# Graph network with edge lists on one core: when the edge stages fetch and put, and which queues carry four of the transfers

## The chip, the cores and the metric

The kernel runs on one core of a Trainium2 chip. The metric is the device time of one execution in microseconds. Three runs of the kernel before took 3205.14, 3216.49 and 3216.53 us; the median is 3216.49 us.

The engines are TensorE (PE, with PEld for its weight loads), VectorE (DVE), ScalarE (ACT), GpSimd (POOL) and SyncE (SP). SP computes nothing here; it issues transfers. A transfer is issued by an engine, in the order of that engine's instructions, so an instruction that has to wait holds up the transfers behind it.

## The reference

32 entries x of 512 nodes by 256 features pass through four layers. `adj` is a 512 by 512 matrix in which about 1.6% of the cells and the diagonal are not zero; it is the same for all entries. Layers 0 and 3 are the same function with other weights:

```
pre_u, pre_v = h @ W1[:d], h @ W1[d:]
S   = sigmoid(relu(pre_u[u] + pre_v[v] + b1) @ W2 + b2)      # 512 x 512 pairs (u, v)
a_t = (S * adj).T @ h
m_t = (adj @ h) * h
z   = beta1*h + beta2*(a_t @ Wa + ba) + beta3*(m_t @ Wm + bm)
```

Layer 1 is `z + relu(adj @ z @ W.T + b)`. Layer 2 is attention: `feats = y @ W1.T`, one number f1 per node, `coefs = softmax(leaky_relu(f1[i] + f1[j]) + adj)`, and `coefs @ feats + bias2 + y`.

S is wanted only where `adj` isn't zero, since it is multiplied by `adj`. This is what the kernel uses.

## The kernel before, in words

The kernel counts the cells of `adj` and takes `sparse_path` where they fit into fixed lists, as they do here. The 32 entries are worked on in 8 groups of four (`NB = 4`, t = 0 to 7). Each group passes through these pieces of work, each of which is a Python generator that yields between its parts:

- `first` (layer 0, four entries in turn): loads h (512 KB), transposes it on PE (`turned`), writes the transposed entry hT to `xT` in device memory, and calls `pre` four times an entry, on blocks of 128 nodes. One `pre` multiplies by W1 on PE, adds b1 on DVE (L548), copies the other half on ACT (L549), computes the pair (u, u) of the diagonal on DVE (L551, L552), and sends the block `puv`, 256 KB, to a table in device memory (L556). The send is held back by one block (`settle`).
- `edges` (layer 0 or 3): the pairs (u, v) of all four entries. There are 36 items of 128 pairs. For an item, GpSimd gathers 128 rows of 4 KB from the table by an indirect transfer (`fetch`, L581) into `rows`, a ring of five buffers. DVE adds `mine` to it, the other end of the pair (L653), and then, for each of the four entries, applies relu, multiplies by W2 and sums (L666). Every fourth item exp on ACT and the rest of the sigmoid on DVE follow; then each item's values of S are scattered by GpSimd into `cells` in device memory (`put`, L575, one an item). `cells` is in two halves; puts into the same half follow each other's landing. S on the diagonal leaves through two transfers of SP (L605). The first fetches (`lead` of them: 3, or with spare buffers 4 in the first stage and 5 in the last) stand in front of the items in one piece, without a yield between them; puts that are left after the last item stand in one piece behind it.
- `middle` (layers 0, 1 and 2): `load` brings S back from `cells` as a dense matrix, four transfers of 1 MB on SP (L688) into the tiles `SA0`. For each entry the sums of layer 0 (L801 and after), layer 1 (whose last addition on DVE, L877, gives yT), the attention of layer 2, the result transposed to `x2T` (L879) and, transposed back on PE and copied by ACT, as `x2` (L891, two transfers an entry), and `pre` for layer 3, which fills layer 3's table.
- `last` (layer 3): S again through `load` (tiles `SA3`), products with Wa (`hWa`), with `adj` (`mhT`), and the sums (L948, L957, L960) to the output.

The order of work is written down in `sparse_path` as a list of streams: each generator has a stretch of time, in units of one group's period, and shares of it. `weave` (L442) sorts all pieces by these planned times and runs the generators in that order, which is the order in which instructions are recorded. Streams of the kind "fill" (`first`, `last`) aren't run at their time but held in a list, and taken from it where `middle` says that PE has room. From t = 2 on, `first` of a group is planned at start − 0.8 to start − 0.54, its layer 0 `edges` at start − 0.53 to start − 0.05, `middle` from start to start + 1, layer 3's `edges` from there for 0.48, and `last` at end + 0.52 to end + 1.2. A scheduler then gives each engine its own list, and may move an instruction past others that it doesn't depend on. So in a steady period DVE works through the edges of layer 0 of the next group, then those of layer 3 of this one, while PE does `middle`, `first` and `last`.

The table of layer 0's edges must be complete before the first gather of `edges`, and S must be scattered completely before `load`.

Of the kernel before, what the change touches and what calls it, by code (L numbers as in the profile page):

```python
# [16 lines left out]
P = 128  # L17
N = 512
D = 256
NC = N // P  # L20
# [10 lines left out]
LINES = PANELS * P  # L31
LEAD = 3
CELLS = HALF * N
ITEMS = NC * OWN + 2 * PANELS
# [378 lines left out]
class Sparse:  # L413
# [28 lines left out]
    def weave(self, streams):  # L442

        order = []
        for k, (_, shares, a, b, _) in enumerate(streams):
            at = 0.0
            for j, share in enumerate(shares):
                order.append((a + (b - a) * at / sum(shares), k, j))  # L450
                at += share
        due, running = [], set()

        def run(k, j):
            g, shares = streams[k][:2]
            room = next(g, None)
            if j == len(shares) - 1:
                for _ in g:
                    raise AssertionError("more pieces than told")
            return room  # L460

        def fill(upto):
            while len(due) > upto:
                run(*due.pop(0))

        for _, k, j in sorted(order):
            kind, end = streams[k][4], len(streams[k][1]) - 1
            if kind == "fill":
                due.append((k, j))
                fill(HELD if running else 0)  # L470
                continue
            if kind == "main" and j == 0:
                running.add(k)
            elif j == 0 and kind != "free":
                fill(0)
            if run(k, j) and due:
                fill(len(due) - (1 if len(due) < HELD // 2 else 2))
            if kind == "main" and j == end:
                running.remove(k)
        fill(0)  # L480
# [104 lines left out]
    def edges(self, g, spare=()):  # L585
# [6 lines left out]
        ready, fetched = [], {}  # L592
        lead = LEAD + len(spare) - 1 if spare else LEAD
        tags = [None] * 5 + list(spare)
# [3 lines left out]
        def own_1():  # L598
# [3 lines left out]
            for q in range(2):  # L602
                diagonal = g.cells[q][q * HALF : q * HALF + HALF * (N + 1), :]
                diagonal = diagonal.rearrange("(c p a) b -> p c a b", p=P, a=N + 1)[:, :, 0, :]
                nc.sync.dma_start(diagonal, g.self_s[:, 2 * q : 2 * q + 2, :])  # L605

# [36 lines left out]
        for n in range(lead):  # L643
            fetch(n)
        yield

# [29 lines left out]
        for _, f in todo:  # L676
            f()
        while ready:
            put()
        yield  # L680

    def load(self, g, layer):

        tiles = []
        for c in range(NC):
            t = self.act.tile([P, N, NB], F32, name=f"SA{layer}", bufs=NC)
            cells = g.cells[c // 2][c % 2 * P * N : (c % 2 + 1) * P * N, :]
            self.nc.sync.dma_start(t.rearrange("p v b -> p (v b)"), cells.rearrange("(p v) b -> p (v b)", p=P))  # L688
            tiles.append(t)
# [26 lines left out]
    def first(self, g, i):  # L716
# [8 lines left out]
        for b in range(NB):  # L725
            ahead = load(b + 1) if b < NB - 1 else None
            hT = self.turned(h, "hT0", "hT")
            yield
            self.nc.sync.dma_start(self.xT[i + b], hT)
            yield from self.pre(g, b, hT)  # L730
# [55 lines left out]
    def middle_one(self, g0, g3, b, i, SA, keep, given):  # L786
# [96 lines left out]
        for c in range(0, NC, 2):  # L883
# [6 lines left out]
            nc.scalar.copy(x2, by_two(pt))  # L890
            nc.sync.dma_start(self.x2s[i][:, c : c + 2, :], x2)  # L891
            yield
# [93 lines left out]
def even(n):  # L986
    return [1.0] * n
# [3 lines left out]
FIRST, LAST, AHEAD, BEHIND = even(NB * 5 + 1), even(NB * 8 + 1), even(NB * 4 + 1), even(NB * 4 + 1)  # L991
EDGES = [4.0] + even(ITEMS + 1)

# [17 lines left out]
def sparse_path(ctx, m, counts, xr, outr, B):  # L1011
# [4 lines left out]
    streams = [  # L1016
        (sp.setup(), even(NC + 1 + NC + 2 * (OWN // 2 + 1) + 1), -0.40, -0.295, ""),
        (sp.setup_behind(), even(2 * (OWN // 2 + 1) + 2 * PANELS + 4), -0.285, -0.16, ""),
        (sp.setup_rest(), even(7), -0.26, -0.20, ""),
        (sp.zeros_behind(), even(2), 0.15, 0.2, ""),  # L1020
    ]
    for t in range(last + 1):
        g0, g3 = Group(sp, m.g0, f"0_{t}"), Group(sp, m.g3, f"3_{t}")
        start, end = (max(0.0, k - 0.47) for k in (t, t + 1))
        behind = (end, end + 0.48), (end + 0.52, end + 1.2)
        if t == 0:
            early = (-0.385, -0.30), (-0.292, -0.02)
        elif t == 1:
            early = (-0.28, -0.06), (0.02, start - 0.04)
        else:  # L1030
            early = (start - 0.8, start - 0.54), (start - 0.53, start - 0.05)
        if t == last - 1:
            behind = (end, end + 0.46), (end + 0.6, end + 1.08)
        if t == last:
            end -= 0.2
            behind = (end, end + 0.46), (end + 0.29, end + 0.45)
        streams += [
            (sp.first(g0, t * NB), FIRST, *early[0], "fill"),
            (sp.edges(g0, ("yT", "mhT3") if t == 0 else ()), EDGES, *early[1], ""),
            (sp.middle(g0, g3, t * NB), middle_shares(t == 0), start, end, "main"),  # L1040
            (sp.edges(g3, ("yT", "h1", "hT1") if t == last else ()), EDGES, *behind[0], "free"),
        ]
        if t == 0:
            streams.append((sp.middle_before(g0, 0), AHEAD, -0.15, -0.03, ""))
        if t < last:
            streams.append((sp.last(g3, t * NB), LAST, *behind[1], "fill"))
        else:
            streams.append((sp.last_before(g3, t * NB), AHEAD, *behind[1], ""))
            streams.append((sp.last_behind(g3, t * NB), BEHIND, end + 0.5, end + 0.6, ""))
    sp.weave(streams)  # L1050
# [237 lines left out]
```

## Time and profile before

| | |
|---|---|
| three runs | 3205.14, 3216.49, 3216.53 us; median 3216.49 |
| profiled execution, its own time | 3222.47 us |
| its span | 3220.7 us |
| mean granted TensorE clock | 0.924 |
| PE busy | 2741.7 us (85%) |
| DVE busy | 2351.1 us (73%) |
| POOL busy | 1472.2 us (46%) |
| ACT busy | 980.4 us (30%) |
| moved by DMA | 679.37 MB, mean 211 GB/s |
| gathers of rows (L581) and scatters of S (L575) on POOL | 554 of mean 1.21 us, 576 of mean 1.18 us |
| S loads on SP (L688) | 64 of 1 MB, median 7.0 us from issue to landing |
| table writes on SP (L556) | 256 of 256 KB, median 4.7 us |
| xT written (L729), x2T written (L879), on SP | 32 and 32 of 512 KB, median 6.8 and 4.5 us |

A line of the profile's table of groups reads: program line, engine, operation, tile written, an arrow, tiles read, how many; then busy microseconds and the mean of one in nanoseconds; then how long the engine stood idle just before such an instruction and what ended the largest part of that. In the table of waits, the three numbers are idle microseconds, how many waits, and the longest. In the chain, each row has its start, its length, and who it was; it is followed back from the last instruction, each step to whatever released it.

Stages can be told apart in the trace by the gathers: a stage begins when the first rows are fetched after its table has been written. The layer 0 stages begin at about 649, 1024, 1401.8, 1774.3, 2150 and 2522 us, the layer 3 stages at about 850, 1223, 1600, 1975, 2349 and 2720 us. Before 505 us lie the building of the lists and the first group's start, and from 3015 us the last group's end.

### The profile page before, as it was taken

How to read it: one execution, taken by the hardware profiler on the slowest of the kernel's cores; microseconds unless marked ns; L12 is line 12 of the kernel's file. 1: busy time of each engine (PE TensorE's matmuls, PEld its weight loads, DVE VectorE, ACT ScalarE, POOL GpSimd, SP SyncE). 2: the span in 40 equal slices, each digit the busy share in tenths (PEclk: the TensorE clock that was granted, in tenths of full speed). 3: DMA queues.
4: the chain of work that ended last, by engine and by line, in shares of the span. 5: the costliest groups of instructions: out<-in, count | busy, mean ns of one | idle time of the engine just before them, and what ended most of it. 6: DMA issues, size and time to landing. Idle time of an engine off the chain costs nothing.

```text
span 3220.7 us, 32267 instructions
## 1 busy us (share of the span) xinstructions
PE 2741.7 (85%) x8645; PEld 1652.4 (51%) x8646; DVE 2351.1 (73%) x7594; ACT 980.4 (30%) x2309; POOL 1472.2 (46%) x1248
## 2 busy tenths in 40 slices
PE   6356888889997998979998899979989799989947
PEld 3123444446553665545654565535655466545636
DVE  7677837988595967969497785959678694962672
ACT  4352333322233222322223222332223222232441
POOL 1565504546263644627264462636445372540371
PEclk9677988999998999989999999989999899999979
DMA  8876526886777656786577766776567775751663
GB/s 274 295 241 214 174 92 214 260 254 194 223 226 252 206 190 207 233 255 220 176 227 246 223 202 206 229 247 201 193 210 241 258 225 176 223 169 39 201 211 111
DMA packets 302716, 679.37 MB, mean 211 GB/s; under 512 B 52672, under 2 KB 170944, under 8 KB 294336
## 3 DMA queue, kind: packets, MB, share of 16 engines
q0 software_dynamic: 111168, 338.90, 33.9%
q1 hardware_dynamic: 186224, 334.68, 31.6%
q10 hardware_dynamic: 5136, 3.68, 0.4%
q8 instruction: 70, 1.15, 0.2%
q14 instruction: 118, 0.97, 0.1%
HBM read 531.12 MB, written 146.01 MB: 210 GB/s over the span
## 4 chain that ended last, share of the span: by engine, by line
PE 35%; DVE 27%; DMA 12%; issue 5%; ACT 2%; POOL 1%; SPq 0%; DVEq 0%; ACTq 0%; POOLq 0%
PE pst L43 24%; DVE rows L666 9%; DVE rows L653 8%; DMA rows<-table,iv 5%; PE pst L948 4%; DMA table<-puv 3%; PE pst L801 2%; DMA cells<-s,cell 2%; PE pst L899 2%; PE pst L957 1%; DVE ex L855 1%; DMA mine<-table,iu 1%; PE pst L808 1%; DVE both L551 1%; DVE puv L548 1%
## 5 line engine op out<-in xcount | busy, mean ns | idle before, releaser
L581 POOL DMA_INDIRECT rows<-table,iv x554 | 671.2, 1212 | 1060.3 <-DMA table<-puv 392.8
L575 POOL DMA_INDIRECT cells<-s,cell x576 | 678.6, 1178 | 587.0 <-DMA cells<-s,cell 348.2
L653 DVE TENSOR_TENSOR rows<-rows,mine 128x1024 f32<-128x1024 f32 x554 | 667.6, 1217 | 185.5 <-DMA rows<-table,iv 158.0
L666 DVE SCALAR_TENSOR_TENSOR rows<-rows,L_gnn_W2bc 128x256 f32<-128x256 f32 x2016 | 749.4, 416 | 0.4
L43 PE MATMUL pst<-adj,h 128*128 128x512 f32 x1024 | 452.6, 593 | 0.0
L43 PE MATMUL pst<-L_gnn_Wa,hT 128*128 128x256 f32 x1024 | 274.1, 423 | 131.6 <-DMA hT<-xT 75.9
L43 PE MATMUL pst<-w_L_gnn_W,hT 128*128 128x512 f32 x512 | 259.2, 644 | 79.0 <-ACT hT L536 74.0
L43 PEld LDWEIGHTS pst<-L_gnn_Wa,hT 128*128 128x128 f32 x1024 | 216.5, 217 | 176.4 <-issue 104.6
L43 PEld LDWEIGHTS pst<-adj,h 128*128 128x128 f32 x1024 | 192.9, 191 | 221.2 <-issue 218.8
L43 PE MATMUL pst<-w_L_gnn_W,yT 128*128 128x512 f32 x512 | 240.5, 623 | 44.9 <-DVE yT L877 44.9
L43 PE MATMUL pst<-eT,feats 128*128 128x512 f32 x512 | 233.8, 611 | 9.4 <-ACT eT L900 9.4
L43 PE MATMUL pst<-adjT,zW 128*128 128x512 f32 x512 | 225.0, 593 | 0.0
L948 PE MATMUL pst<-hWa,SA 128*128 128x256 f32 x896 | 217.2, 398 | 0.0
L948 PEld LDWEIGHTS pst<-hWa,SA 128*128 128x128 f32 x896 | 213.8, 328 | 6.0 <-issue 3.3
L549 ACT COPY puv<-pst 128x256 f32<-128x256 f32 x256 | 94.7, 372 | 391.3 <-DVE puv L548 367.7
L548 DVE TENSOR_TENSOR puv<-pst,bc_L_gnn_b 128x256 f32<-128x256 f32 x256 | 107.0, 418 | 137.6 <-PE pst L43 81.9
L43 PEld LDWEIGHTS pst<-w_L_gnn_W,hT 128*128 128x128 f32 x512 | 101.9, 207 | 191.5 <-issue 94.2
L801 PE MATMUL pst<-flat,hWa 128*128 128x512 f32 x448 | 197.2, 593 | 1.3 <-DVE both L551 1.3
L43 PEld LDWEIGHTS pst<-w_L_gnn_W,yT 128*128 128x128 f32 x512 | 102.4, 201 | 175.2 <-issue 110.1
L770 ACT COPY flat<-SA 128x512 f32<-128x512 f32 x128 | 134.7, 1124 | 182.6 <-PE pst L43 111.4
L899 PE MATMUL pst<-ident,ex 128*128 128x128 f32 x512 | 97.1, 329 | 105.7 <-DVE ex L860 59.5
L566 ACT ACTIVATE s<-s,L_gnn_nb 128x16 f32<-128x16 f32 (+2 forms) x176 | 53.5, 304 | 411.4 <-DVE rows L666 399.6
(165 smaller groups left out, 3696.4 us busy)
## 6 DMA issues: line engine op xcount, KB each, us to landing
table<-puv SPq DMA_DIRECT2D x256, 256.0 KB, 4.7
SA<-cells SPq DMA_DIRECT2D x64, 1024.0 KB, 7.0
h<-in_x_dram SPq DMA_DIRECT2D x64, 512.0 KB, 6.1
mine<-table SPq DMA_DIRECT2D x64, 512.0 KB, 5.4
hT<-xT SPq DMA_DIRECT2D x36, 512.0 KB, 4.6
h<-x2s SPq DMA_DIRECT2D x36, 512.0 KB, 5.3
xT<-hT SPq DMA_DIRECT2D x32, 512.0 KB, 6.8
x2T<-yT SPq DMA_DIRECT2D x32, 512.0 KB, 4.5
```

Source lines behind the costliest of these rows:

```text
L43: nc.tensor.matmul(out, lhsT, rhs, start=(n == 0), stop=(n == len(pairs) - 1))
L548: nc.vector.tensor_tensor(puv[:, 0, :], pp[:, 0:D], w["b1bc"], ALU.add)
L549: nc.scalar.copy(puv[:, 1, :], pp[:, D:])
L566: self.nc.scalar.activation(t, t, AF.Exp, bias=w["nb2"], scale=-1.0)
L575: self.nc.gpsimd.indirect_dma_start(out=g.cells[half], out_offset=bass.IndirectOffsetOnAxis(ap=at, axis=0), in_=s, in_offset=None)
L581: self.nc.gpsimd.indirect_dma_start(out=rows, out_offset=None, in_=g.table, in_offset=bass.IndirectOffsetOnAxis(ap=at, axis=0))
L653: nc.vector.tensor_tensor(rows, rows, other, ALU.add)
L666: nc.vector.scalar_tensor_tensor(part, part, 0.0, w["W2bc"], ALU.max, ALU.mult, accum_out=at)
L770: self.nc.scalar.copy(flat[:, r, :], SA[r][:, :, b])
L801: nc.tensor.matmul(pz, hWa[:, r, cs], flat[:, r, :], start=(r == 0), stop=False)
L899: nc.tensor.transpose(pt[:, js], ex[:, js], self.m.ident)
L948: nc.tensor.matmul(pz[:, k * D : (k + 1) * D], SA[r][:, cs, b], hWa[:, r, :], start=(r + k == 0), stop=False)
```

## The change

1. `edges` yields after each of the first fetches, and after each of the puts that are left at its end (`TAIL` of 6), so that `weave` gives each a planned time of its own (`edge_times`): the first fetches of a stage are planned between the last items of the stage before, the last puts between the first items of the next.
2. With spare buffers, `lead` is 5 in the first and in the last stage.
3. `first` of a group is planned 0.06 of a period earlier, and `last` from end + 0.56 to end + 1.13 instead of end + 0.52 to end + 1.2.
4. The diagonal's two transfers (L605) and the S loads (L688) are issued by GpSimd instead of SP.
5. hT is written to `xT` (L729), and x2 (L891), by ScalarE instead of SP.

`weave` now takes the list of planned times of each stream; `spread` computes it from shares as before. The line numbers in the text are those of the kernel before.

```diff
+LEAD_AT_ENDS = 5
+TAIL = 6
...
-        lead = LEAD + len(spare) - 1 if spare else LEAD
+        lead = LEAD_AT_ENDS if spare else LEAD
...
-                nc.sync.dma_start(diagonal, g.self_s[:, 2 * q : 2 * q + 2, :])
+                nc.gpsimd.dma_start(diagonal, g.self_s[:, 2 * q : 2 * q + 2, :])
...
         for n in range(lead):
             fetch(n)
-        yield
+            yield
...
         for _, f in todo:
             f()
+        for _ in range(TAIL - 1):
+            put()
+            yield
         while ready:
             put()
         yield
...
-            self.nc.sync.dma_start(t.rearrange("p v b -> p (v b)"), cells.rearrange("(p v) b -> p (v b)", p=P))
+            self.nc.gpsimd.dma_start(t.rearrange("p v b -> p (v b)"), cells.rearrange("(p v) b -> p (v b)", p=P))
...
-            self.nc.sync.dma_start(self.xT[i + b], hT)
+            self.nc.scalar.dma_start(self.xT[i + b], hT)
...
-            nc.sync.dma_start(self.x2s[i][:, c : c + 2, :], x2)
+            nc.scalar.dma_start(self.x2s[i][:, c : c + 2, :], x2)
...
-EDGES = [4.0] + even(ITEMS + 1)
+def edge_times(ahead, a, b, behind, lead=LEAD):
+    step = (b - a) / ITEMS
+    first = [ahead + j * min(step, (a - ahead) / lead) for j in range(lead)]
+    return first + spread(even(ITEMS), a, b) + spread(even(TAIL), b, behind)
...
-        behind = (end, end + 0.48), (end + 0.52, end + 1.2)
...
+            first = spread(FIRST, -0.385, -0.30)
+            edges0 = edge_times(-0.292, -0.27, -0.03, -0.02, LEAD_AT_ENDS)
...
-            early = (start - 0.8, start - 0.54), (start - 0.53, start - 0.05)
+            first = spread(FIRST, start - 0.86, start - 0.6)
+            edges0 = edge_times(start - 0.552, start - 0.505, start - 0.06, start - 0.04)
+        edges3 = edge_times(end + 0.003, end + 0.05, end + 0.48, end + 0.54)
+        behind = end + 0.56, end + 1.13
...
-            behind = (end, end + 0.46), (end + 0.29, end + 0.45)
+            edges3 = edge_times(end + 0.003, end + 0.02, end + 0.45, end + 0.46, LEAD_AT_ENDS)
+            behind = end + 0.29, end + 0.45
```

## The prediction

> **What bounds the kernel now.** I read first the page's busy shares and chain.
>
> ```profile
> PE 2741.7 (85%) x8645; PEld 1652.4 (51%) x8646; DVE 2351.1 (73%) x7594; ACT 980.4 (30%) x2309; POOL 1472.2 (46%) x1248
> PE 35%; DVE 27%; DMA 12%; issue 5%; ACT 2%; POOL 1%; SPq 0%; DVEq 0%; ACTq 0%; POOLq 0%
> ```
>
> No engine bounds alone: PE and DVE take turns, joined by DMA latency. A group recurs every 373 us (an `edges` stage for layer 0 starts at 1401.8, 1774.3, 2150). So second I took busy time in 15 us stretches of one such start (columns: sum and count for PE, PEld, DVE, ACT, POOL; granted clock; DMA share; GB/s).
>
> ```profile
> 1730.00:1745.00 15.00, 12.95 (x43) 7.32 (x42) 11.68 (x48) 4.64 (x13) 7.04 (x7) 0.89 0.35 91
> 1745.00:1760.00 15.00, 7.06 (x18) 3.30 (x18) 7.01 (x22) 5.64 (x13) 3.42 (x3) 0.69 0.87 316
> 1760.00:1775.00 15.00, 14.27 (x53) 8.56 (x52) 7.26 (x27) 6.36 (x15) 0.66 (x1) 0.96 0.87 273
> 1775.00:1790.00 15.00, 5.64 (x14) 2.43 (x13) 3.88 (x10) 4.09 (x4) 4.10 (x5) 0.83 1.08 274
> 1790.00:1805.00 15.00, 15.00 (x36) 6.82 (x36) 12.88 (x47) 3.34 (x8) 4.29 (x3) 0.83 0.72 229
> ```
>
> From 1745 to 1790 both engines are half idle. Third, the chain through it:
>
> ```profile
> 1736.90 6.28 PE pst L43 x12
> ...
> 1743.35 8.07 DMA table<-puv
> 1751.51 0.42 DVE puv L548
> ...
> 1769.44 4.63 DMA table<-puv
> 1774.07 0.26 issue
> 1774.34 12.48 DMA rows<-table,iv
> 1786.84 1.24 DVE rows L653
> ...
> 1788.88 0.68 DVE yT L877
> 1789.60 8.19 PE pst L43 x12
> ```
>
> The last item of the stage before ends at 1737.8. The next stage's first must wait for `first` to write its table (to 1774.1), then for a gather (12.5 us). The gap is 49 us. Inside it DVE stalls for a `puv` buffer, because the table write behind the S loads lands after 8.07 us instead of the page's 4.7. At its end PE waits 9.4 us for the second x2T half (L877), queued on DVE behind that first item. Fourth, the waits:
>
> ```profile
> POOL cells L575 <- DMA cells<-s,cell: 348.2, 155, 8.4
> DVE puv L548 <- DMA table<-puv: 55.3, 14, 8.8
> SPq L688 <- DMA cells<-s,cell: 325.0, 30, 26.1
> ```
>
> Scatters to one half queue behind each other's landing. SP stands 325 us at S loads that wait for scatters. The other start (layer 3, 1600 us) is different: from 1481 to 1600 the chain is PE without a break, so idle DVE there costs nothing.
>
> [...] DMA share is 1.08 at 1775 with SP and POOL both feeding it. [...] So S loads leave the table writes' queue and enter the gathers'. The page's queue table shows q0 and q1 apart[...]. [...]
>
> **The change, part by part.** The order in which the built kernel issues tells more than the diff. Per group, against before:
>
> 1. *`first` earlier.* DVE has 5 blocks of `pre` left after the last item instead of 10. Five blocks of three 0.42 us operations (L548, L551, L552), 6.3 us, move ahead of that item; two sums additions (L960, 0.68 us each) leave. So the last item comes 5 us later, DVE and PE both being full there.
> 2. *The gap.* One of two batches is gone, with its buffer stall (6.5 us on DVE). Last item to last block: turned batch, 4 blocks at 1.72 us of PE (6.9 for 16 records) and softmax in between, some 14 us; table write 4.6: table ready 18 us after the last item, an estimate. But POOL must pass its last scatters first. In the built order they still stand ahead of the first fetches, and now three of the four S loads with them; the third waits for the last landing. Before, the four serial scatters began 4.1 us after the last item and the last began at 20.1. S loads now in the same ring may slow them, a wait on the scatter before the first S load adds 1 to 4 us. I take the fetch at 20 to 24 after the last item (36.5 before), so POOL and not the table gates it. Landing: 7.6 us at the quiet start (1600.35), 12.5 here; I take 10, with an S load just ahead. First item at 30 to 34 instead of 49: gain 15 to 19, central 17.8.
> 3. *x2T behind three items.* Before, one addition stood between the two halves. Now three additions (1.22 us each), ten of L666 (0.35 apart) and the first half precede the second half: 3.7 + 3.5 + 0.7, and its own 0.7; PE resumes 8.5 us after the first item starts, not 2.8: +5.7.
> 4. *`last` earlier.* Half a batch of sums, 16 records of L948 (3.7 us) and a few of L957 (0.2 each), moves from the new group's first batch into the batch that ends `middle`, PE-bound: +4.4; DVE running ahead takes back about 2.5 of the PE waits on softmax (L860, 11 us a group). Net +1.9.
> 5. *Diagonals on POOL.* Two per start, ahead of the fetches at the quiet start. POOL shows no plain DMA; the nearest row is the 1.0 us scatter. They are ready at 1598.0 and the table lands at 1600.1: 0.3 us, at most 3 if each takes 2. S loads likewise 1 to 2 us, behind idle POOL; without that idle time, 8 us a group.
> 6. *hT and x2 from ACT.* 12 issues a group at SP's 0.35 to 0.5 us: 5 us on an engine 30% busy. Some stand before the next `puv` copy[...]: 0.5 to 2 us, I take 1.2. SP gains the time; its waits hide behind PE and DVE otherwise.
> 7. *Tail spread, fetches spread*: mostly undone by the issue order, 0 (−1 to +1).
> 8. *Lead 5 instead of 4 in the first stage*: DVE waits 32 us for gathers before 520 us; a quarter, −8 (0 to −15). The last stage already has 5. At the end the S loads follow the last scatters through one queue: +6 (2 to 10).
>
> Group: +5 −17.8 +5.7 +1.9 +0.3 +1.2 = −3.7. Six starts: −22; ends −2: −24. The profiled execution (3222.5, span 3220.7) would become 3198; the median of the runs shown, 6 us lower at 3216.5, 3192.
>
> **Rivals.** *A, the forecast (0.45)*: the shorter gap outweighs what is put in front of x2T and PE. For: 49 us of half-idle engines. Against: it is a difference of large terms.
>
> *B, an even trade (0.20)*: PE's work per group is unchanged and its idle time only some 38 of 373 us; the buffer stall goes and the x2T wait grows by as much. The gap gains 14: ±0, 3216.
>
> *C, slower (0.30)*: POOL's queue becomes the bound at the layer 0 start. S loads of 1 MB each put themselves between the last serial scatters and ahead of the gathers. Before, scatters beside S loads took 5.5 and 6.7 us to land:
>
> ```profile
> 1747.46 0.96 POOL L575 DMA_INDIRECT cells<-s,cell  x1 [4.59 <-DMA cells<-s,cell]
> 1754.18 1.42 POOL L575 DMA_INDIRECT cells<-s,cell  x1 [5.76 <-DVE puv L548]
> ```
>
> If three take 7 and the S load before the fetch 4 us, the fetch starts at 30 and lands at 42: gain 7, group +7, six +42, ends +8: 3266. It decides once the first item comes later than 35 us after the last one (gain below 14). Against: the puts' loads overlap in the old order as well.
>
> *D, it does not do what it says (0.05)*: fetches keep behind the puts, and the batch moved forward only shifts the last item: within 0.5%.
>
> **How the numbers follow.** The runs shown spread by 0.35%, and 0.5%, 16 us, is about what a measurement can tell. A alone spans 3140 to 3210: gains of 23 (quiet landing, table as gate) to 15. Of A 0.43 lies below 3200; of B and D 0.06 below, 0.14 within, 0.05 above; C has 0.01 below, 0.02 within, 0.27 above, with A's other 0.02 within. So faster 0.50, same 0.18, slower 0.32. The range 3138 to 3270 takes in C at its likely size and A at its best; A's own is 3140 to 3210.
>
> **What would show it.** In the changed profile: the time from the last L653-type addition of one stage to the first of the next at a layer 0 start, 30 to 34 us (above 35 is C); `DVE puv <- DMA table` well below 55; SP's wait at S loads gone and POOL waiting at them instead; the PE wait for x2T at 12 to 15 us, not 9.4; no longer gap at the layer 3 start. The prediction is wrong if POOL's S loads take several us each, if DVE starves for rows inside the stages because gathers share their ring[...].

## The result and the profile after

The kernel after takes 3212.62 us (median of 12 runs, 3206.76 to 3220.60); the kernel before, run beside it, 3215.51 us (12 runs, 3203.09 to 3221.36). The ratio is 1.000, 95% interval 0.9985 to 1.0015: no difference. The forecast was 3192 us.

The profiled execution of the kernel after spans 3216.7 us, that of before 3220.7. In both, the work is cut by the first gather of each edge stage into a start (to the third layer 0 stage), four whole groups, and an end:

| us | before | after | difference | forecast |
|---|---|---|---|---|
| first gather of the layer 0 stage at 1000 us | 1024.2 | 1001.4 | −22.8 | −8 |
| four groups from there (one group) | 1498.3 (374.6) | 1497.8 (374.5) | −0.5 (−0.1) | −14.8 (−3.7) |
| last layer 0 stage to the next first gather | 200.0 | 206.1 | +6.1 | in "six starts" |
| from there to the last stage's first gather | 295.7 | 297.0 | +1.3 | in "six starts" |
| last stage to the end of the span | 202.5 | 214.4 | +11.9 | +6 |

So a group, which was to gain 3.7 us, gained nothing. Inside a group, as the mean of the five layer 0 starts from the one at 1000 us on and of the four layer 3 starts between them (gap: from the end of the last row addition of one stage to the start of the first of the next; stage: from the start of its first row addition to the end of its last):

| us in a group | before | after | difference |
|---|---|---|---|
| gap ahead of layer 0's stage | 51.1 | 38.8 | −12.3 |
| in it: first gather issued after | 39.6 | 32.4 | −7.2 |
| in it: gather to first addition | 11.5 | 6.5 | −5.0 |
| layer 0's stage | 126.9 | 137.5 | +10.6 |
| gap ahead of layer 3's stage | 69.0 | 67.6 | −1.4 |
| layer 3's stage | 127.6 | 130.9 | +3.3 |

The gap did shrink, and the stages beside it grew by as much. PE stood still for 17.8 us of the gap before and for 15.3 us of it after: of the 12.3 us that the gap lost, PE had worked through all but 2.5. The page's busy times and the chain's shares, of the kernel after:

```profile
PE 2740.0 (85%) x8646; PEld 1646.8 (51%) x8646; DVE 2344.3 (73%) x7594; ACT 976.4 (30%) x2309; POOL 1526.4 (47%) x1344
PE 36%; DVE 31%; DMA 21%; issue 6%; ACT 3%; POOL 2%; SPq 0%; POOLq 0%; ACTq 0%; DVEq 0%
```

The work of PE and DVE is what it was; in the chain, transfers have gone from 12% to 21%. The start of a layer 0 stage in stretches of 15 us (the same columns as in the prediction), which lies 23 us earlier than the one shown of before:

```profile
1706.00:1721.00 15.00, 14.09 (x47) 7.73 (x46) 14.57 (x64) 5.63 (x15) 9.29 (x8) 1.00 0.71 244
1721.00:1736.00 15.00, 11.18 (x39) 6.89 (x38) 12.30 (x42) 8.70 (x21) 4.61 (x5) 0.89 0.85 269
1736.00:1751.00 15.00, 9.09 (x28) 4.44 (x26) 0.00 (x0) 5.49 (x7) 3.50 (x4) 0.95 0.40 140
1751.00:1766.00 15.00, 2.25 (x3) 1.17 (x4) 8.03 (x25) 0.00 (x0) 8.63 (x9) 0.50 0.83 279
1766.00:1781.00 15.00, 15.00 (x37) 6.69 (x36) 8.87 (x31) 2.87 (x7) 3.26 (x4) 0.87 0.82 244
```

Before, both engines were half idle for 45 us. Now the batch of `pre` and the softmax that filled part of this are done by 1735, and what is left is a hole: DVE runs nothing at all from 1736 to 1751, PE almost nothing from 1751 to 1766, and the granted clock is at 0.50 there. The chain through it:

```profile
1732.46 5.92 DMA cells<-s,cell
1738.65 5.13 DMA cells<-s,cell
...
1744.53 2.21 DMA cells<-s,cell
...
1747.48 2.11 DMA cells<-s,cell
...
1751.35 1.00 POOL rows L580
...
1753.90 7.88 DMA rows<-table,iv
1761.81 1.23 DVE rows L652
1763.03 0.66 DVE yT L879
...
1765.81 0.67 DVE yT L879
...
1770.20 8.76 DMA table<-puv
```

Four scatters follow each other's landing, then come the gathers, then three row additions on DVE, and behind them both halves of x2T, for which PE waits (L879 here is L877 of before). What the chain leaves out is what stood ahead of the four. POOL before and after (the first and the last of the four before; after, also two of the S loads):

```profile
1741.90 0.96 POOL L575 DMA_INDIRECT cells<-s,cell  x1 [0.60 <-DVE both L551]
...
1757.91 1.04 POOL L575 DMA_INDIRECT cells<-s,cell  x1 [2.31 <-DMA cells<-s,cell]
```

```profile
1731.58 0.57 POOL L690 DMA_DIRECT2D SA<-cells  x1 [4.96 <-DMA cells<-s,cell]
1732.46 1.19 POOL L574 DMA_INDIRECT cells<-s,cell  x1 [0.30 <-DVE cols L859]
...
1747.48 0.97 POOL L574 DMA_INDIRECT cells<-s,cell  x1 [1.99 <-DMA cells<-s,cell]
1750.13 0.57 POOL L690 DMA_DIRECT2D SA<-cells  x1 [1.68 <-DMA cells<-s,cell]
```

As the mean of the five starts, counted from the end of the last item (which comes 3.0 us after its row addition before, 1.9 after), the first of the four leaves at 3.9 us before and at 10.8 after, the last at 20.3 and 26.8. So the four take no longer among themselves, 16.4 and 16.0 us; they begin 6.9 us later, as the first S load now stands ahead of them and waits 1.7 to 5.8 us for a landing. The third S load then puts 3.6 us between the last of them and the first gather, which leaves at 30.4.

Whether the table was there is told by SyncE, which loads `mine` from it, and by PE's own line:

```profile
1734.27 0.85 SPq L620 DMA_DIRECT2D mine<-table  x2
```

```profile
1763.75 2.93 PE L45 MATMUL pst<-w_L_gnn_W,yT 128*128 128x512 f32 x3 [17.94 <-DVE yT L879]
```

The table is complete at 1734.3, the first gather leaves POOL at 1751.4: 17 us in which only POOL's queue holds it. PE stands 17.9 us, and then runs slowly: its first eight records come 0.85 us apart (the first two 1.0), the later ones 0.43.

The page's waits that the prediction had named:

```profile
POOL cells L574 <- DMA cells<-s,cell: 379.7, 170, 7.1
DVE rows L652 <- DMA rows<-table,iv: 286.2, 52, 23.3
DVE puv L547 <- DMA table<-puv: 65.2, 23, 7.8
```

The wait for scatters rose (348.2 before), DVE's for gathers rose from 158.0, and the wait for a `puv` buffer, which was to fall well below 55, is 65.2: at 1770 it stands behind the x2T wait instead of inside the gap.

Last, PE's waits over three steady groups (first gather to first gather, 1401.8 to 2522.5 before):

```profile
PE pst L899 <- DVE ex L860: 34.8, 15, 5.5
PE pst L43 <- ACT hT L536: 33.0, 9, 8.5
PE pst L43 <- DVE yT L877: 28.0, 3, 9.4
PE pst L43 <- DVE hT L809: 10.5, 6, 2.8
```

and after, 1375.3 to 2499.2:

```profile
PE pst L45 <- DVE yT L879: 51.6, 3, 18.0
PE pst L901 <- DVE ex L862: 26.0, 12, 3.9
PE pst L45 <- DVE hT L811: 21.6, 10, 4.4
PE pst L45 <- DVE yT L830: 5.5, 4, 2.5
PE pst L45 <- ACT hT L535: 4.4, 6, 1.3
```

A group: the earlier tables took 9.5 us from PE's wait for hT and 2.9 from that for the softmax, and gave 7.9 to x2T, 3.7 to the sums' end (hT, L811) and 1.8 to yT (L830). With the small ones, PE waits 36.5 us a group before and 38.7 after. Take these waits from the group's 373.6 and 374.6 us (the mean of these three), and 337 and 336 us are left, PE's own work; in the runs below it is 333 to 340. Such a sum can be made for every engine, since each works or waits: DVE works 288 to 290 us of a group in all runs and waits for the rest. PE's is the useful one because it has the least left over and each of its waits has a name. That a DVE gap costs only what PE waits in it is not shown by the sum, but by runs below in which one of the two changes and the other doesn't.

### The profile page after: what moved, and what is told of

Its sections match the earlier page's. It is cut to its first block, busy times and chain, and to the rows that moved or that the text cites. A ratio compares the mean times of both kernels' runs of the same rounds, so it can differ in the third digit from the quotient of the medians.

```text
span 3216.7 us, 32210 instructions
## 1 busy us (share of the span) xinstructions
PE 2740.0 (85%) x8646; PEld 1646.8 (51%) x8646; DVE 2344.3 (73%) x7594; ACT 976.4 (30%) x2309; POOL 1526.4 (47%) x1344
## 3 DMA queue, kind: packets, MB, share of 16 engines
q0 software_dynamic: 121408, 406.15, 39.3%
q1 hardware_dynamic: 154480, 233.88, 21.8%
q10 hardware_dynamic: 18960, 37.24, 3.2%
## 4 chain that ended last, share of the span: by engine, by line
PE 36%; DVE 31%; DMA 21%; issue 6%; ACT 3%; POOL 2%; SPq 0%; POOLq 0%; ACTq 0%; DVEq 0%
PE pst L45 25%; DVE rows L665 10%; DVE rows L652 10%; DMA rows<-table,iv 6%; DMA table<-puv 5%; DMA cells<-s,cell 4%; PE pst L950 4%; PE pst L959 2%; PE pst L803 2%; DMA mine<-table,iu 2%; PE pst L901 2%; DVE ex L857 1%; ACT flat L772 1%; DVE mhT L713 1%; POOL rows L580 1%
## 5 line engine op out<-in xcount | busy, mean ns | idle before, releaser
L45 PE MATMUL pst<-L_gnn_Wa,hT 128*128 128x256 f32 x1024 | 266.4, 413 | 121.9 <-DMA hT<-xT 59.2
L45 PEld LDWEIGHTS pst<-L_gnn_Wa,hT 128*128 128x128 f32 x1024 | 209.2, 210 | 169.7 <-issue 52.6
L45 PE MATMUL pst<-w_L_gnn_W,hT 128*128 128x512 f32 x512 | 251.6, 629 | 13.6 <-ACT hT L535 12.0
L45 PE MATMUL pst<-eT,feats 128*128 128x512 f32 x512 | 232.2, 607 | 11.5 <-ACT eT L902 11.5
L45 PE MATMUL pst<-WT,hT 128*128 128x256 f32 x512 | 148.4, 447 | 61.1 <-DVE hT L811 60.9
L604 POOL DMA_DIRECT2D cells<-self_s x32 | 24.0, 758 | 361.1 <-DVE self_s L600 220.5
L901 PE MATMUL pst<-ident,ex 128*128 128x128 f32 x512 | 90.6, 317 | 98.8 <-DVE ex L862 61.5
```

What stands on the lines that cost most here:

```text
L45: nc.tensor.matmul(out, lhsT, rhs, start=(n == 0), stop=(n == len(pairs) - 1))
L901: nc.tensor.transpose(pt[:, js], ex[:, js], self.m.ident)
```

## The experiments

Each ratio is to the kernel before on the same chip, with its 95% interval. "Group" is the mean of four groups from the layer 0 stage near 1000 us on, "start" the time of that stage's first gather, "PE waits" the mean of three groups, and in it the wait for x2T; all from one profile each. A profiled execution lies up to 14 us from the median of its kernel, 1.6 us a group if that is spread evenly (an estimate), so smaller differences of the last columns are not told. "Group" leaves out the start and the end of the kernel; "times only", for one, loses 13 us after the last steady group.

| kernel | ratio | group | start | gap | PE waits (x2T) |
|---|---|---|---|---|---|
| before | | 374.6 | 1024 | 51.1 | 36.5 (9.3) |
| after | 1.000 | 374.5 | 1001 | 38.8 | 38.7 (17.2) |
| times only | 0.9976 (0.9965 to 0.9987) | 368.3 | 1019 | 35.3 | 32.2 (14.5) |
| queues only | 1.0069 (1.0040 to 1.0098) | 376.2 | 1019 | 52.8 | 39.5 (15.6) |
| after, S on SP | 0.9981 (0.9965 to 0.9997) | 372.5 | 1005 | 37.2 | 38.2 (9.6) |
| after, diagonal on SP | 1.0015 (1.0003 to 1.0027) | 373.3 | 1009 | 42.3 | 40.0 (19.7) |
| after, S and diagonal on SP | 0.9945 (0.9927 to 0.9964) | 366.8 | 1018 | 33.9 | 32.4 (7.2) |
| after, xT and x2 on SP | 1.0061 (1.0037 to 1.0085) | 375.6 | 1009 | 35.8 | 39.5 (15.3) |
| before, diagonal on POOL | 1.0020 (1.0007 to 1.0033) | 374.0 | 1015 | 50.8 | 38.4 (8.9) |
| times only, tables as before | 1.0079 (1.0039 to 1.0119) | 376.3 | 1025 | 53.1 | 39.0 (7.4) |
| S and diagonal on SP, tables at −0.89 | 1.0127 (1.0100 to 1.0153) | 377.9 | 1031 | 38.4 | 43.4 (8.7) |
| after, tables at −0.92 | 1.0138 (1.0098 to 1.0177) | 383.9 | 1001 | 28.2 | 44.9 (0) |
| times only, panels turned | 1.0056 (1.0036 to 1.0075) | 376.0 | 1015 | 38.5 | 41.9 (20.9) |
| S, diagonal on SP, first three diagonals on POOL | 0.9941 (0.9922 to 0.9960) | 369.1 | 1006 | 37.9 | 34.8 (9.7) |
| after, last scatters behind gathers | 0.9874 (0.9837 to 0.9911) | 365.0 | 998 | 22.8 | 28.6 (2.0) |
| after, x2T first | 0.9820 (0.9796 to 0.9843) | 363.2 | 1011 | 40.2 | 27.5 (0) |
| S, diagonal on SP, x2T first | 0.9831 (0.9808 to 0.9853) | 361.6 | 1015 | 37.4 | 27.4 (0) |
| the same, last scatters behind gathers | 0.9781 (0.9760 to 0.9802) | 360.6 | 1003 | 29.1 | 27.2 (0) |
| before, x2T first | 0.9946 (0.9926 to 0.9967) | 368.5 | 1021 | 51.3 | 31.3 (0) |

### Times and queues apart

"Times only" is the kernel after with the four kinds of transfers back on SyncE:

```diff
-nc.gpsimd.dma_start(diagonal, ...
+nc.sync.dma_start(diagonal, ...
-self.nc.gpsimd.dma_start(t.rearrange("p v b -> p (v b)"), ...
+self.nc.sync.dma_start(t.rearrange("p v b -> p (v b)"), ...
-self.nc.scalar.dma_start(self.xT[i + b], hT)
+self.nc.sync.dma_start(self.xT[i + b], hT)
-nc.scalar.dma_start(self.x2s[i][:, c : c + 2, :], x2)
+nc.sync.dma_start(self.x2s[i][:, c : c + 2, :], x2)
```

> The kernel after with all four kinds of transfers on SyncE again: only the planned times and the fetches one by one are left. Theory P (POOL's queue, with serial scatters and S loads, gates the layer 0 fetch, and each us of the gap is on the path): without S loads in POOL's queue the first fetch comes 28 to 30 us after the last row addition instead of 32, gap 35 us, 3190 to 3200 us. Theory Q (the gap's work is only moved: what the gap loses the next stage gains): the gap may shrink by 3 us, the layer 0 stage grows by as much, 3207 to 3218 us.

"Queues only" is the kernel before with the same four lines the other way round.

> The kernel before with only the four queue changes. Theory P: the table, ready 36 to 39 us after the last row addition, is later than POOL's queue (32), so the gap stays 51 us and the time 3212 to 3225 us. Rival C of the prediction (S loads hold up POOL): gap above 55 us, 3240 us or more. Theory Q: 3210 to 3222 us, the same as before.

The times alone are worth 6.3 us a group, on a gap of 35.3; the time, 3204 us beside 3212, lies between the two theories. The queues alone cost 0.7%, 3232 us, which no theory had: the gap is 52.8, not the 55 of rival C, and PE's wait for x2T has grown from 9.3 to 15.6. Then one queue at a time. S loads alone back on SP (the third and fourth line above):

> The kernel after with only the S loads back on SyncE's queue. Theory P: the first layer 0 fetch 28 to 30 us after the last row addition instead of 32 (three S loads less ahead of it, and no wait for a landing before them), 3192 to 3202 us. Theory Q: 3207 to 3218 us with a longer layer 0 stage. If S loads ahead of the fetch are what was mis-sized, most of the missing 5 us of the gap come back here.

The fetch moved as theory P said, from 32.4 to 28.2 us, and the gap by only 1.6, since the gathers landed 2.6 us later: S loads on SP then run beside them. The four scatters do leave earlier, at 4.7 to 20.5 us after the last item instead of 10.8 to 26.8, but in four of the five starts the gather then waits 4.4 to 6.5 us more, for the table: on SP the S loads, which wait for scatters, hold up the table's last writes instead. So the queue that carries the S loads decides which of the two gates the gather. 2 us a group, 3208 us against 3212, below what P expected. xT and x2 alone back on SP (the last four lines):

> The kernel after with xT and x2 written from SyncE's queue again (S loads and diagonal still from GpSimd). Theory X [...]: the steady period falls from 374.5 to 371 us or less. Rival D (the diagonal on GpSimd costs it): period 374 to 376. Both: if xT's writes from ScalarE are what shortened the start (the fifth stage's first fetch at 1001 us, 1019 with the queues of before), it is at 1010 us or later here. Time 3195 to 3205 us under X, 3212 to 3225 under D.

Theory X, that the writes cost time when ScalarE issues them, falls: the group is 375.6 us, and the time, 3240 us, is above both ranges on a chip on which the kernel before takes 3221. The writes from ScalarE don't cost; by the ratios (1.0061 here, 1.000 with them, on another chip) they help by 0.6% of the time, 7 us of it ahead of the steady groups. S loads and diagonal back on SP:

> The kernel after with S loads and the diagonal on SyncE's queue again, xT and x2 still from ScalarE: against the run with only S loads moved back (period 372.5 us) it moves the diagonal alone. Theory D: period 369 us or less, time 3192 to 3202 us. Theory X: period 372 to 374 us, time 3205 to 3212 us.

This one is 0.55% faster than before, group 366.8 us: theory D by its group, with 3204 us just above D's range. But the diagonal alone back on SP (the first two lines) gains nothing:

> The kernel after with the diagonal alone on SyncE's queue again (S loads stay on GpSimd, xT and x2 on ScalarE). Theory D (the diagonal on GpSimd costs 5.7 us a period, S loads 2.0, and they add): period 374.5 - 5.7 = 369 us, start (first fetch of the third layer 0 stage after 1000 us) at 1014 to 1020 instead of 1001, ratio to before 0.995 to 0.998. Rival (the diagonal costs only together with S loads on SyncE): period 373 us or more, ratio 1.000 to 1.004.

and alone on POOL, in the kernel before, it costs nothing in the group:

> The kernel before with the diagonal alone on GpSimd. Theory D, as a price of the queue itself: period 374.6 + 5.7 = 380 us, start 10 to 15 us earlier, ratio 1.004 to 1.010. Rival O (the price comes from the order in which the scheduler then leaves the other engines' work, which depends on the whole plan): period 373 to 377 us, ratio 0.996 to 1.002.

So the diagonal has no price of its own (rival O holds: 374.0 us, the ratio at the edge of its range). (The letters are those of the expectations; theory D is not the prediction's rival D.) Either of the two on GpSimd brings the group from 366.8 to about 373, both to 374.5. By PE's waits, S loads on POOL go with 17.2 to 19.7 us for x2T and 9 for the softmax, S loads on SP with 7.2 to 9.6 and 14 to 16. What the diagonal changes beside S loads on SP, 38.2 us of waits to 32.4, is spread over x2T (2.4), softmax (2.0) and smaller ones. Why two small transfers of 4 KB count here only beside S loads on SP is not settled.

### The place of the tables

```diff
-first = spread(FIRST, start - 0.86, start - 0.6)
+first = spread(FIRST, start - 0.92, start - 0.66)
```

> The kernel after with the layer 0 tables planned 0.06 of a period earlier still (start - 0.92 to start - 0.66). In the built order four gathers then stand ahead of the third S load and of the last two scatters. Theory P: first fetch 24 us or less after the last row addition, gap 30 us or less, the stretch in which DVE and PE both stand still shorter by 8 us, 3155 to 3180 us. Theory Q: the last item comes later and the layer 0 stage longer by what the gap loses, 3207 to 3222 us.

The gap fell to 28.2 us as theory P said, PE waited for no x2T, and the kernel was 1.4% slower, 3256 us, above both theories. Back to the place of before, with times only:

> The kernel with only the planned times changed, but the layer 0 tables planned at start - 0.8 to start - 0.54 as before (layer 3's last step still earlier, and gathers and scatters one by one). If the earlier tables are what gives the 6 us a period: period back to 374 us, first fetch 36 us or more after the last row addition, time 3210 to 3225 us. If the earlier last step gives it: period 369 us or less, 3200 to 3208 us.

All of the gain of "times only" goes, and 1.7 us more, 3252 us: it was the earlier tables, and what is left of the new times costs 0.8% without them. Half way to −0.92, on S and diagonal on SP:

> The same best kernel so far with the layer 0 tables planned 0.03 of a period earlier (start - 0.89), half way to the place that cost 9 us a period with all queues changed (start - 0.92). If the loss grows evenly from start - 0.86: period 370 to 373 us, ratio 1.000 to 1.005. If start - 0.86 is on a flat part: period 365 to 368 us, ratio 0.992 to 0.997.

A loss of 11 us a group for 11 us of shift, much more than even growth. Its PE waits, over three groups, and one start of it:

```profile
PE pst L901 <- DVE ex L862: 75.4, 13, 14.5
PE pst L45 <- DVE yT L879: 26.0, 3, 11.2
```

```profile
1772.96 0.42 DVE L547 TENSOR_TENSOR puv<-pst,bc_L_gnn_b 128x256 f32<-128x256 f32 x1 [10.42 <-DMA table<-puv]
1774.83 1.11 PE L901 MATMUL pst<-ident,ex 128*128 128x128 f32 x4 [13.30 <-DVE ex L862]
```

25 us a group for softmax parts, where the run that it changes ("after, S and diagonal on SP") has 13.8: the whole loss. At each layer 0 start a block of `pre` now stands ahead of the softmax on DVE, and waits 10.3 to 11.3 us for a `puv` buffer, that is for a table write. At −0.92 it is a row addition that stands there and waits 11.7 to 15.3 us for its gather, and PE's wait for the softmax has grown as well, from 8.7 us to 23. A shorter gap is no gain by itself; the work taken out of it comes to stand in front of something else that PE needs.

### What gates the gather, with no work moved

Theory P needed a run in which the gather comes earlier and nothing else moves. First try, on "times only": the last four scatters go into one half of the cells; with the panels turned, they alternate.

```diff
-tail = [panel_of(h, q) for h in range(2) for q in range(PANELS)]
+tail = [panel_of(h, q) for h in (1, 0) for q in range(PANELS)]
```

> The kernel with only the planned times changed, and the four panels' order turned round, so that the last scatters of a stage alternate between the two halves of the cells instead of going four times into one. Theory P (what holds the first gather, once its table is there, is on the path): last scatter and first fetch 6 to 10 us earlier after the last row addition (fetch 19 to 23 us), and as no work is moved ahead of it, period 362 to 365 us, time 3160 to 3185 us. Theory Q (the period is set by the work of PE and DVE, not by the hole): period 367 to 369 us, time 3198 to 3210 us, a longer layer 0 stage.

Slower, 376.0 us a group instead of 368.3. The scatters were done 9 us earlier, but SyncE shows what came instead (columns: start, length, line, transfer):

```profile
1746.48 0.48 SPq L620 DMA_DIRECT2D mine<-table  x1
1757.90 0.33 SPq L690 DMA_DIRECT2D SA<-cells  x1
1758.32 1.23 SPq L555 DMA_DIRECT2D table<-puv  x2
...
1766.53 1.41 SPq L690 DMA_DIRECT2D SA<-cells  x3
```

and POOL:

```profile
1759.00 0.96 POOL L574 DMA_INDIRECT cells<-s,cell  x1 [1.41 <-DMA cells<-s,cell]
1766.94 0.98 POOL L580 DMA_INDIRECT rows<-table,iv  x1 [6.98 <-DMA hT<-x2T]
```

The first S load needs the other half, whose last scatter now comes late; it holds SP for 10.9 us, until 1757.9, with the last two table writes behind it. The table became the gate, and the other three S loads left SP together with the gathers, which took 13.0 us to land. Second try, an order of issue: each scatter left at the end of a layer 3 stage behind the last first gather of the next layer 0 stage (on the kernel after).

```diff
 for _ in range(TAIL - 1):
-    put()
+    with self.tc.issue_after(self.lead_ins) if g.behind else nullcontext():
+        put()
     yield
```

> The kernel after, with an order of issue added on GpSimd: the last scatters of a layer 3 stage stand behind the first gathers of the next layer 0 stage, as the change's plan has it and the built order hasn't. No work of PE or DVE is moved for it. Theory P (POOL's queue gates the start and this is on the path): first fetch 20 us or less after the last row addition (32 in the kernel after, with the table there at 16 to 17), period 360 to 367 us, ratio 0.973 to 0.987. Theory Q: the fetch comes as early, the layer 0 stage is longer by as much, period 372 to 376 us. Rival K (collision: scatters and S loads now run beside the gathers): landing of the first rows 10 us or more instead of 6.5, period 375 us or more.

POOL in this run:

```profile
1708.68 1.05 POOL L574 DMA_INDIRECT cells<-s,cell  x1 [0.30 <-issue]
1729.49 0.99 POOL L580 DMA_INDIRECT rows<-table,iv  x1 [19.76 <-issue]
...
1734.32 1.00 POOL L574 DMA_INDIRECT cells<-s,cell  x1 [0.31 <-issue]
```

The first gather leaves 16.9 us after the last addition, as the table lands, and the scatters follow. The gap is 22.8 us, the landing 5.9 (no collision, rival K falls), PE's wait for x2T 2.0, the group 365.0: 1.3% faster. Theory P holds, with the ratio at the edge of its range. This is what the change's plan says and its built order doesn't do.

### Who waits behind the gather

The other way: the gather stays late, but x2T doesn't stand behind it. On DVE, the first eight row additions of a layer 0 stage are issued after both halves of x2T (on the kernel after).

```diff
-nc.vector.tensor_tensor(rows, rows, other, ALU.add)
+with self.tc.issue_after(self.x2T_ins) if k < 8 and g.held else nullcontext():
+    nc.vector.tensor_tensor(rows, rows, other, ALU.add)
```

> The kernel after, with an order of issue added: at each layer 0 start from the third group on, the two halves of x2T stand ahead of the first eight row additions on DVE (items planned at start - 0.472). In the kernel after PE waits there 17 us a period, as both halves stand behind additions that wait for the gathers. Theory W (this PE wait is on the path): it falls below 4 us, period 360 to 366 us instead of 374.5, ratio to before 0.973 to 0.985. Theory Q (PE's and DVE's work sets the period, the wait only turns up elsewhere): the wait falls too, but period 371 to 375 us, ratio 0.995 to 1.002.

(The items are planned at start − 0.472 here instead of start − 0.505, so that x2T is recorded ahead of them, and its second half is issued after its first; this holds from the third group on. The later place alone was not run; the last run of this section has the order without it.) The gap is 40.2 us, no shorter than in the kernel after, but PE stands for only 5.9 us of it instead of 15.3, and the group falls by 11.3 us to 363.2: 1.8% faster than the kernel before. PE's waits over three groups (L881 is x2T here, and has no row left):

```profile
PE pst L45 <- DVE hT L812: 24.5, 13, 4.4
PE pst L45 <- DVE both L550: 18.6, 3, 7.6
PE pst L904 <- DVE ex L863: 18.6, 11, 2.6
```

Theory W holds, and Q falls: the wait was on the path. Of the 17.2 us taken away, 6.2 return as a wait for `both` (L550), which reads a block of `pre` out of PSUM. The same on S and diagonal on SP:

> The kernel after with S loads and the diagonal on SyncE (0.9945 so far, period 366.8), and x2T ahead of the first additions of a layer 0 stage. Its PE wait at that place is 7 us a period, so theory W gives a period of 360 to 363 us and a ratio of 0.983 to 0.990; theory Q 365 to 368 us, 0.992 to 0.997.

and with the scatters behind the gathers as well:

> The same as the run before it, with the last scatters of a layer 3 stage behind the first gathers as well (S loads on SyncE). Theories W and P together: fetch 20 us or less after the last addition, period 353 to 360 us, ratio 0.970 to 0.983. Theory Q: 365 to 368 us, 0.992 to 0.998. Rival K: landing 10 us or more, period 368 us or more, above 0.998.

The first has the theory's numbers (361.6 us, 0.9831). The second doesn't add up to W and P: with x2T first, the earlier gather is worth 1.0 us a group by these profiles (by the medians the two are 12.8 us apart, but the first one's profile is its fastest run, 8 us below its median). Its rows lie ready, the gap is 8 us shorter, and the first addition now waits for x2T, that is for PE: the 12.2 us from gather to addition are this and not rival K's landing. It is the fastest of all, 3159 us beside 3231, 2.2% faster than the kernel before on that chip. Queues matter little once x2T stands first: 363.2 with S loads and diagonal on POOL, 361.6 on SP (0.9820 and 0.9831 by time), where the difference was 7.7. Last, the same edit on the kernel before:

> The kernel before with x2T ahead of the first eight row additions of a layer 0 stage, nothing else. PE waits there 9.3 us a period in the kernel before (17.2 after). Theory W (that wait is on the path in both): period 374.6 - 6 to 9 = 366 to 369 us, ratio 0.984 to 0.991; the kernel after with the same edit reached 363.2 us and 0.982, so the change itself would then be worth 3 to 6 us a period. If the change is worth nothing even without this wait: 362 to 364 us, 0.980 to 0.983. If the wait is on the path only where the gather is late as in the kernel after: 373 to 376 us, 0.997 to 1.002.

The group falls by 6.1 us of the 9.3 that PE waited there, inside theory W's range; the time falls by 0.5%, less than expected from it. In part this is the choice of executions: this profile is the fastest of its eight runs, 7.2 us below their median, and that of the kernel before lies 7 us above its own. The kernel after with the same edit has 5.3 us less a group than this one, and 1.3% less time by the ratios: that is about what the change, with its items planned later, is worth where it doesn't lengthen the wait for x2T.

### The start

Runs with the diagonal on POOL and the new times reached the layer 0 stage near 1000 us up to 17 us earlier than those without (1001 us against 1018; there is also 1009 on either side). On the version with S loads and diagonal on SP:

```diff
-nc.sync.dma_start(diagonal, ...
+(nc.gpsimd if g.early else nc.sync).dma_start(diagonal, ...
+g0.early, g3.early = t < 2, t < 1
```

> The kernel after with S loads and the diagonal on SyncE (the best so far, 0.9945), but the diagonal of the first three edge stages on GpSimd. If the 13 to 17 us by which runs with the diagonal on GpSimd reach the third layer 0 stage earlier belong to these stages: that fetch at 1000 to 1006 us instead of 1018, period 367 us, ratio 0.989 to 0.991. If not: 1015 to 1020 us, ratio 0.993 to 0.996.

The start is 12 us shorter, 1006 instead of 1018, so the gain belongs to these stages; but in this profile the groups are 2.3 us longer: the first addition comes 9.8 us after the gather instead of 6.7, and PE's wait for x2T is 9.7 us instead of 7.2. Why is open, and the ratio, 0.9941, is not to be told from 0.9945.

## Why the prediction was wrong

The time lay in the range, 3138 to 3270, but the gain of 24 us, with 0.50 on faster, did not come. Rival B, an even trade, is nearest: of the 12.4 us that PE no longer waits for hT and the softmax, the wait for x2T takes 7.9 and the waits for hT (L811) and yT (L830) 5.5. The stall for a `puv` buffer, which B had going, only moved. By the prediction's steps:

- **1, the last item later**: +5 expected, +3.3 measured (the layer 3 stage). Right.
- **2, the gap**: this is the term that failed first. −17.8 expected, −12.3 measured. That POOL and not the table gates the gather was right; its time was not: 20 to 24 us after the end of the last item expected, 30.4 measured. The serial scatters were not slowed (16.0 us from the first to the last of the four, 16.4 before). What made it late is what the prediction names but didn't size: the wait at the first S load, 1 to 4 us taken and 1.7 to 5.8 measured, stands ahead of the four scatters, which start 6.9 us later than before; and the third S load behind the last scatter, which has no number in the sum, takes 3.6 us. The range of 20 to 24 left no room for both above the 20.1 us at which the last scatter had left before. Rival C had the gather at 30 us, which is right, and its landing at 12, which is not: the first addition came 6.5 us after it (10 taken in the forecast).
- **2 again, its weight**: this failed too. The prediction entered the whole gap as gain, on DVE's clock, and PE's wait as one more term. PE stood for 17.8 us of the gap before and for 15.3 after, so that 12.3 us less of gap were 2.5 for PE. The run with x2T first gains 11 us with a gap as long as that of the kernel after, and the tables at −0.92 lose 9 with a gap 11 us shorter.
- **3, x2T behind three items**: the place was right, the size not. +5.7 expected, 12 to 15 us of wait; 17.2 measured, +7.9, as the first half too stands behind the additions and the additions behind the late gather. The two terms are one: a gather later than estimated holds PE as well as DVE. The run with x2T first shows it to be on the path.
- **4, `last` earlier**: +1.9 expected. Not measured alone; all new times but the earlier tables cost 1.7 us a group and 0.8% of the time. The layer 0 stage grew by 10.6 us where steps 3, 4 and 6 had 8.8; the waits for hT (L811) and yT (L830) were in no step.
- **5, diagonal and S loads on POOL**: 0.3 us a start and 1 to 2 behind idle POOL. An issue takes 0.75 us of POOL for a diagonal and 0.58 for an S load (medians of 32 and 64 in the kernel after); the 2 us at most for a diagonal was the author's estimate. For the kernel after no worse than that: 1.2 and 2.0 us a group. That both on SP would gain 7.7 was not in it; with x2T first it is 1.6 us, and nothing by the time.
- **6, xT and x2 from ACT**: +1.2 expected, the author's estimate, where an issue takes 0.33 us of ScalarE (median, 96 in the kernel after); putting them back costs 0.6% of the time, and in the group 1.1 us, too little to tell. Wrong in sign.
- **7, fetches and tail**: "mostly undone by the issue order" was right, and what it undid is worth 9.5 us a group (the scatters behind the gathers).
- **8, the ends**: the start gained 22.8 us (8 expected), part of it by the diagonal on POOL in the first stages; the end lost 11.9 (6 expected). The last layer 0 stage lost 6.1, since it has the longer stage and no shortened gap after it.

What the prediction watched for: the first addition 30 to 34 us after the last, measured 38.8 (above 35: C); `puv` well below 55, measured 65.2; PE's wait 12 to 15, measured 17.2; SP free of waits for S loads and POOL waiting instead: so it was, 325.0 us on SP gone and 45.0 on POOL; no longer gap at the layer 3 start: so it was, 67.6 us after 69.0. Of its signs of being wrong the first came, as POOL stood 1.7 to 5.8 us at the first S load of each start.

The reading that "idle DVE there costs nothing" at layer 3's start was made on the chain, which is PE's from 1481 to 1600 but for some 6 us of softmax and 5 us at its end; no run tests it.

Not tried: the diagonal alone with other places in POOL's order, which would tell why it counts only beside S loads on SP.

## What to carry to other kernels

Before pricing a gap on one engine, add up what the busiest engine waits in it: here PE, with 336 us of work and 36 to 39 of waits in a group, stood for 18 us of a gap of 51 us on DVE, and for 15 when the gap was 39. In an in-order queue, as SP's here (it held two table writes 10.9 us behind an S load), ask what stands behind an instruction whose operand comes by a slow transfer: two instructions for PE behind row additions for which a gather was late cost more than the gather (11.3 us a group with x2T first, 9.5 with the gather early). A planned place is not a place in the built order; where a scheduler decides, bind the two or three instructions that matter by an order of issue, and compare the order that each engine got.

## What the runs showed of the hardware

- After a standstill of 17.9 us PE's first eight records of 512 columns came 0.85 us apart (the first two 1.0) and the later ones 0.43, and the granted clock was 0.50 from 1763.8 to 1769.8 and 1.00 from there to 1781. In the kernel before, four to eight records at 0.85 us follow the waits of 7.9 to 10.1 us, of which a group has two, where the kernel after has one longer wait; the granted clock was 0.50 to 0.56 in the 5 us behind seven of these eight waits, and 0.50 in the 2.5 us behind the other. So these waits of PE cost more than their length; the prediction had left this out of what the x2T wait costs.
- Scatters of S into one half, each waiting for the landing of the one before, were issued 6.2 and 5.9 us apart beside two S loads of 1 MB, and then 3.0 apart: from 1744 to 1750 the transfers moved 1 GB/s at a DMA share of 0.01, so that what is left there is a latency, not bandwidth.
- The first addition of a layer 0 stage came 5.5 to 6.8 us after the issue of its gather where at most one S load was issued within 1.2 us of it (the kernel after and the run with the scatters behind the gathers), 9.0 to 10.9 where two were (four starts of "after, S on SP"), and 11.8 to 13.8 where three were ("times only, panels turned"). In the kernel before, with no S load but three or four other loads of 512 KB issued within 2.1 us, it was 10.6 to 12.5.
- With the S loads issued by GpSimd the page's queue q0, which has the gathers (554 of 512 KB, 290 MB) and scatters, carried 406.15 MB instead of 338.90 (64 loads of 1 MB are 67.1 MB), and q10, with xT and x2 from ScalarE, 37.24 instead of 3.68; q1, SyncE's, fell from 334.68 to 233.88. So the S loads did come into the gathers' queue, as the prediction had it.
